# A graph network's first edge pass: three steps between the stages of the mixing, and products two tiles ahead of their sums

## The chip, the cores and the metric

One core of a Trainium2 chip runs the whole program. The metric is device time in microseconds for one execution. TensorE is called PE, VectorE DVE, ScalarE ACT, GpSimd POOL and SyncE SP, as in the profile.

## The reference, cut to what matters

Two layers over 3125 nodes with 256 features. Layer 0 is a max over edges, plus a linear attention ("mixing"), plus two chosen experts out of eight:

```python
xn = _layernorm(x)
# graph part: theta(x_dst - x_src) + phi(x_src), relu, segment_max over edges
e = relu((xn[dst] - xn[src]) @ theta_w.T + theta_b + xn[src] @ phi_w.T + phi_b)
gnn = segment_max(e, dst)
# mixing
q, k, v = split(xn @ W_qkv + b_qkv);  q2 = (q - mean(q))**2;  k2 = (k - mean(k))**2
k2 = l2norm_over_nodes(k2 / (sum(k2) + 1e-7));  q2 = l2norm(q2 / (sum(q2) + 1e-7))
mix = (v + q2 @ (k2.T @ v) / sqrt(N)) @ W_out + b_out
x = x + gnn + mix
x = x + layernorm(expert_mixture(layernorm(x)) + layernorm(x))
```

Layer 1 sums edges by relation, has another attention and another mixture of experts. The change does not touch it.

## The kernel before, in words

The nodes are 25 tiles of 128 rows, with the feature side transposed in `xT`. The program builds edge lists (to about 172 us), runs the first edge pass (172 to 1379 us), makes tables per relation, runs a second edge pass and ends with the experts of layer 1.

**The first edge pass** (`edge_pass`, line 1336, called at line 1956). For each tile POOL issues 22 to 45 indirect gathers (line 194), each of which brings one neighbour row for 128 nodes, in chunks of four that share one tile `gt` of a pool with six buffers. DVE takes the maximum of what came (line 1368), two rows at a time. The order of the instructions on DVE and POOL is the order in which the code issues them; PE and ACT are ordered by the scheduler.

**Background jobs.** All other work of layer 0 is cut into jobs with a cost each, in the deque `bg`. After each chunk of n gathers a credit grows by rate × n, the rate between 0.9 and 1.3 (what is left of costs over what is left of gathers), and jobs are taken while the credit is above zero. So the costs say only where, between which chunks, the instructions of a job stand. They are not times.

**The mixing.** `mix_tile` is a generator in three stages for each tile. Stage nought: PE projects q, k and v (lines 189, 1766, 1769) into PSUM tiles `mm` (four buffers), ACT copies v with the two means (`vs`, line 1774) and squares q and k with their sums in `ss` (lines 1775, 1776; `ss` is of the pool `small` with six buffers). Stage one: DVE inverts `ss` and scales k (lines 1778 to 1780), ACT squares for the norms (lines 1783 to 1786), PE accumulates `pkv` and `pnk` (lines 1788, 1792). Stage two: DVE scales q (lines 1794 to 1797), PE transposes it (line 1800), ACT copies it to `xt` (line 1801). The job `mix_step(i)` runs stage two of tile i-4, stage one of tile i-2 and stage nought of tile i. `nodes_in` jobs between them normalise the nodes (`xn`, line 172, pool `work` with two buffers) and transpose them (line 183, copied by ACT at 184). `mix_end` closes the mixing and makes `u_mix`.

**Products, sums, norms.** A group of one to three tiles (tiles 1, 2-3, 4-6, 7-9, 10-12, 13-15, 16-18, 19-21, 22-23, 24, then 0) has a `Fin0` object, whose jobs are added when the group's gathers are through. `products(j)` lets PE compute the node's own term into `po` (a tile `pt` of `ps_tr`, two buffers, shared with the transposes) and gnn and mixing terms into `pa` (`mm`). `sums(j)` lets DVE add them up (lines 1868 to 1871), with statistics. `norms` normalises the group (lines 1878 ff.), sums the means in `pmean` and transposes. Then come `hidden` (line 1526, gelu at 1530), `outputs_a` (lines 1552, 1555), `outputs_out` (copies by ACT, lines 1565, 1566) and `outputs_b` (DVE, lines 1574, 1575) of the two experts guessed from the first tiles. Routing (line 1453) and the checks on sorted edges (`redo`, line 1667) are jobs too. Tile 0 comes last and its products are at the end of the pass. "16-0" below is the chunk 0 of tile 16.

Of the kernel before, what the change touches and what calls it, by code (L numbers as in the profile page):

```python
# [11 lines left out]
F32 = mybir.dt.float32  # L12
# [8 lines left out]
P = 128  # L21
D = 256
NN = 3125
NT = 25
# [66 lines left out]
def rows(t):  # L91
    return LAST if t == NT - 1 else P
# [9 lines left out]
def gps_kernel(ctx: ExitStack, tc: tile.TileContext, a, out):  # L102
# [8 lines left out]
    ps_tr = ctx.enter_context(tc.tile_pool(name="ps_tr", bufs=2, space=PSUM))  # L111
    ps_acc = ctx.enter_context(tc.tile_pool(name="ps_acc", bufs=1, space=PSUM))
# [58 lines left out]
    def normalize(dst, src, mv, rs):  # L171
        V.tensor_scalar(dst, src, mv[:, 0:1], rs, op0=ALU.subtract, op1=ALU.mult)  # L172
# [7 lines left out]
    def to_xT(t, src):  # L180
        pt = ps_tr.tile([P, 2, P], F32, name="pt")
        for c in range(2):
            PE.transpose(pt[:, c, :], src[:, c * P : (c + 1) * P], ident)
        S.copy(xT[:, :, t * P : (t + 1) * P], pt)

    def tok_mm(ps, w, t, start=True, stop=True, lhs=None):
        lhs = xT if lhs is None else lhs
        for c in range(2):
            PE.matmul(  # L189
                ps, lhs[:, c, t * P : (t + 1) * P], w[:, c, :], start=start and c == 0, stop=stop and c == 1  # L190
            )
# [763 lines left out]
    with ExitStack() as prx:  # L955
# [204 lines left out]
        for j in range(LT // BLOCK):  # L1160
            pt = ps_tr.tile([P, 2, P], F32, name="pt")
# [157 lines left out]
    def fast():  # L1319
# [100 lines left out]
        pmean = [None]  # L1420
# [167 lines left out]
        with ExitStack() as l0x:  # L1588
# [128 lines left out]
            m0 = m0x.enter_context(tc.tile_pool(name="m0", bufs=2))  # L1717
# [42 lines left out]
            def mix_tile(t):  # L1760
                if t == 0:
                    pnk[0] = ps_acc.tile([P, D], F32, name="pnk", tag="acc1")
                r = rows(t)
                pq = ps_mm.tile([P, 512], F32, name="mm")
                tok_mm(pq, w_qkv[:, :, :512], t, stop=False)
                PE.matmul(pq, ones_row, b_qkv[:, :512], start=False, stop=True)
                pvv = ps_mm.tile([P, 512], F32, name="mm")
                tok_mm(pvv[:, : D + 2], w_qkv[:, :, 512:], t, stop=False)
                PE.matmul(pvv[:, : D + 2], ones_row, b_qkv[:, 512:], start=False, stop=True)
                ss = small.tile([P, 2], F32, name="ss")  # L1770
                q2 = m0.tile([P, D], F32, name="q2", bufs=5)
                k2 = m0.tile([P, D], F32, name="k2", bufs=4)
                vs = m0.tile([P, D + 2], F32, name="vs", bufs=4)
                S.copy(vs, pvv[:, : D + 2])
                S.activation(q2, pq[:, :D], AF.Square, bias=vs[:, D : D + 1], accum_out=ss[:, 0:1])
                S.activation(k2, pq[:, D:], AF.Square, bias=vs[:, D + 1 :], accum_out=ss[:, 1:2])
                yield
                V.tensor_scalar(ss, ss, 1e-7, None, op0=ALU.add)
                V.reciprocal(ss, ss)
                V.tensor_scalar(k2, k2, ss[:, 1:2], None, op0=ALU.mult)  # L1780
                sq = m0.tile([P, D], F32, name="sq")
                s4 = small.tile([P, 1], F32, name="s4")
                S.activation(sq, q2, AF.Square, scale=ss[:, 0:1], accum_out=s4)
                S.activation(s4, s4, AF.Sqrt)
                ksq = m0.tile([P, D], F32, name="ksq")
                S.activation(ksq, k2, AF.Square)
                for c in range(2):
                    PE.matmul(
                        pkv[:, c, :], vs[:r, c * P : (c + 1) * P], k2[:r, :],
                        start=(t == 0 and c == 0), stop=(t == NT - 1), skip_group_check=True,  # L1790
                    )
                PE.matmul(pnk[0], ones[:r, :], ksq[:r, :], start=(t == 0), stop=(t == NT - 1))
                yield
                V.tensor_scalar(s4, s4, 1e-12, None, op0=ALU.max)
                V.reciprocal(s4, s4)
                V.tensor_tensor(s4, s4, ss[:, 0:1], op=ALU.mult)
                V.tensor_scalar(q2, q2, s4, None, op0=ALU.mult)
                pt = ps_tr.tile([P, 2, P], F32, name="pt")
                for c in range(2):
                    PE.transpose(pt[:, c, :], q2[:, c * P : (c + 1) * P], ident)  # L1800
                S.copy(xt_q[:, t, :, :], pt)
# [41 lines left out]

            class Fin0:
                def __init__(self, tiles, accs):
                    self.tiles, self.accs, self.k = tiles, accs, len(tiles)
                    self.mv = small.tile([P, 4, 2], F32, name="mv1")
                    self.rs = small.tile([P, 4], F32, name="rs1")  # L1850
                    self.pa, self.po = {}, {}

                def products(self, j):
                    t = self.tiles[j]

                    po = self.po[j] = ps_tr.tile([P, D], F32, name="pt")
                    tok_mm(po, w_own, t)
                    pa = self.pa[j] = ps_mm.tile([P, 512], F32, name="mm")
                    tok_mm(pa, w_tm, t, stop=False)
                    for c in range(2):  # L1860
                        PE.matmul(
                            pa[:, D:], xt_q[:, t, c, :], u_mix[:, c, :], start=False, stop=False, skip_group_check=True
                        )
                    PE.matmul(pa, ones_row, b_tm, start=False, stop=True)
# [12 lines left out]
                def norms(self):  # L1877
                    V.reciprocal(self.rs[:, : self.k], self.rs[:, : self.k])
                    for j, t in enumerate(self.tiles):
                        if t in (1, SEEN + 1):  # L1880
                            pmean[0] = ps_acc.tile([P, 2], F32, name="pmean", tag=f"acc{1 + (t > 1)}")
                        normalize(xt_tok[:, t, :], x[:, t, :], self.mv[:, j, :], self.rs[:, j : j + 1])
                        V.tensor_tensor(x[:, t, :], x[:, t, :], bet, op=ALU.add)
                        r = rows(t)
                        for c in range(2):
                            PE.matmul(  # L1886
                                pmean[0][:, c : c + 1], xt_tok[:r, t, c * P : (c + 1) * P], ones[:r, 0:1],
                                start=(t in (1, SEEN + 1) and c == 0), stop=(t in (SEEN, 0)),
                                skip_group_check=True,
                            )  # L1890
                        to_xT(t, xt_tok[:, t, :])

                def jobs(self):
                    def step(i):
                        if i < self.k:
                            self.products(i)
                        if i > 0:
                            self.sums(i - 1)

                    out = [(5.0 if 0 < i < self.k else 2.5, lambda i=i: step(i)) for i in range(self.k + 1)]  # L1900
                    return out + [(2.0 * self.k, self.norms)]

            def staged(gen, costs):
# [3 lines left out]
            nodes = [staged(nodes_in(g), (1.0, 4.0) + 5 * (1.2,)) for g in range(5)]  # L1907
            bg.extend(nodes[0])
            mixing = [mix_tile(t) for t in range(NT)]

            def mix_step(i):
                for back in (4, 2, 0):
                    if 0 <= i - back < NT:
                        next(mixing[i - back], None)

            for i in range(NT + 4):
                bg.append((7.0 if i < NT else 3.0, lambda i=i: mix_step(i)))
                if i // 5 + 1 < 5:
                    a0, a1 = ((0, 1), (1, 2), (2, 3), (3, 5), (5, 7))[i % 5]
                    bg.extend(nodes[i // 5 + 1][a0:a1])  # L1920
# [262 lines left out]
        with ExitStack() as l1x:  # L2183
# [126 lines left out]
            class Group:  # L2310
# [174 lines left out]
                def step(self, i):  # L2485

                    self.take()
                    if i < NX:
                        self.hidden(i)
                    if 1 <= i <= NX:  # L2490
                        self.outputs(i - 1)
                    if i == NX + 1:
                        leaving.extend((tick[0] + 9, t) for t in self.tiles)
# [117 lines left out]
    with tc.If(unfit < 1):  # L2611
        fast()
# [78 lines left out]
```

## Time and profile before

| | us |
|---|---|
| median of three runs | 2949.89 |
| the runs | 2949.89, 2947.96, 2967.57 |
| the profiled execution | 2956.36 |
| its span, first to last instruction | 2954.5 |
| mean granted TensorE clock | 0.766 |

Busy time by stretch, in us, from the windows of the trace (POOL counts a gather's own time only):

| stretch, us | PE | DVE | ACT | POOL | granted clock |
|---|---|---|---|---|---|
| 172 to 490, mixing | 191.5 | 135.5 | 76.4 | 199.6 | 0.72 |
| 490 to 1379, rest of the first pass | 434.3 | 341.3 | 85.0 | 569.1 | 0.67 |
| 1379 to 1640 | 218.6 | 148.3 | 53.7 | 104.8 | 0.92 |
| 1640 to 2954 | 960.2 | 509.7 | 287.8 | 745.0 | 0.81 |

In a line of waits, "ss L1778 <- ACT k L1776: 76.2, 8, 21.3" says that the engine stood idle ahead of its instructions of line 1778, that the wait ended with ACT's instruction of line 1776, 76.2 us in 8 times, the longest 21.3. "remote" is a releaser that could not be told by line, "issue" time in which nothing shown was waited for. A line of the timeline has the start, the duration, engine, line, operation, tiles and in brackets the idle time ahead of it.

### The profile page before, as it was taken

The numbers are of one execution on the slowest core, as the hardware profiler recorded it, in microseconds if no ns is written. First come the engines' busy times: TensorE is split into PE (matmuls) and PEld (weight loads), VectorE is DVE, ScalarE is ACT, GpSimd is POOL, SyncE is SP. The second block draws the span as 40 slices with busy tenths as digits, with TensorE's granted clock in tenths as the row PEclk, the third lists the DMA queues.
The fourth block names the chain that finished last, engine by engine and source line by source line (L and its number), as shares of the span: only waits on it lengthen the run. The fifth ranks groups of instructions, "written<-read, shape, count | busy, mean of one in ns | idle before, by whom it ended". The sixth has DMA issues, their size and how long they took to land.

```text
span 2954.5 us, 21207 instructions
## 1 busy us (share of the span) xinstructions
PE 1868.2 (63%) x6161; PEld 1201.3 (41%) x6161; DVE 1227.5 (42%) x3400; ACT 556.2 (19%) x1308; POOL 1718.8 (58%) x1830
## 2 busy tenths in 40 slices
PE   4345666413574635374998267858886886766868
PEld 2223333202342313243443145645554565554657
DVE  7434434434433424334664243335343434343342
ACT  5212221001110101022221122122111122122233
POOL 5566666675667566653146645655666555665651
PEclk9667767655686657687998668878897887887979
DMA  6533333343334233332357432322332222232320
GB/s 180 135 91 86 94 85 104 94 108 101 90 87 107 74 90 85 92 78 58 148 211 237 135 97 75 91 80 84 89 92 85 84 82 79 82 89 73 86 72 18
DMA packets 125963, 290.10 MB, mean 98 GB/s; under 512 B 41386, under 2 KB 63982, under 8 KB 122632
## 3 DMA queue, kind: packets, MB, share of 16 engines
q0 software_dynamic: 83184, 230.02, 28.4%
q1 hardware_dynamic: 38122, 55.88, 5.6%
q10 hardware_dynamic: 4526, 2.71, 0.3%
q8 instruction: 52, 0.85, 0.1%
q14 instruction: 79, 0.65, 0.1%
HBM read 249.07 MB, written 39.41 MB: 98 GB/s over the span
## 4 chain that ended last, share of the span: by engine, by line
PE 25%; issue 9%; another core or an unknown queue 7%; DVE 5%; POOL 4%; ACT 2%; DMA 1%; ACTq 0%; DVEq 0%; SPq 0%; POOLq 0%
PE mm L2432 9%; PE py L2463 7%; PE mm L189 6%; POOL gt L194 4%; DVE gt L1375 1%; PE mm L2326 1%; DVE bnst L163 1%; PE pctx L2271 0%; PE mm L2324 0%; DVE x L2482 0%; PE py L2449 0%; PE pt L2402 0%; DMA gt<-htab_f,idx2g 0%; DVE acc L1377 0%
## 5 line engine op out<-in xcount | busy, mean ns | idle before, releaser
L194 POOL DMA_INDIRECT gt<-htab_f,idx2g x742 | 727.8, 981 | 497.2 <-DVE acc L1377 241.3
L194 POOL DMA_INDIRECT gt<-btab,idx x764 | 751.6, 984 | 389.5 <-issue 208.5
L2432 PE MATMUL mm<-xT,w 128*128 128x256 f32 (+4 forms) x1536 | 429.8, 434 | 107.4 <-issue 61.2
L2463 PE MATMUL py<-w,hT 128*128 128x256 f32 (+1 forms) x1600 | 407.8, 407 | 71.6 <-issue 45.5
L2432 PEld LDWEIGHTS mm<-xT,w 128*128 128x128 f32 x1536 | 294.5, 217 | 224.1 <-issue 121.9
L2463 PEld LDWEIGHTS py<-w,hT 128*128 128x128 f32 (+1 forms) x1600 | 319.8, 203 | 144.1 <-issue 78.9
L1368 DVE TENSOR_TENSOR run<-run,gt 128x512 f32<-128x512 f32 (+1 forms) x400 | 266.3, 666 | 169.6 <-DMA gt<-btab,idx 110.8
L2436 ACT ACTIVATE hT<-mm,b 128x256 f32<-128x256 f32 (+4 forms) x384 | 174.9, 476 | 584.9 <-remote 266.3
L2482 DVE SCALAR_TENSOR_TENSOR x<-py,wf,x 128x256 f32<-128x256 f32 x200 | 88.1, 477 | 440.0 <-remote 226.0
L1375 DVE TENSOR_TENSOR gt<-gt 128x512 f32<-128x512 f32 (+1 forms) x364 | 193.5, 531 | 14.2 <-DMA gt<-htab_f,idx2g 4.9
L1555 PE MATMUL mm<-w,hT 128*128 128x256 f32 x400 | 130.0, 471 | 106.2 <-issue 85.8
L189 PE MATMUL mm<-w_rel,xT 128*128 128x512 f32 x400 | 179.0, 605 | 7.1 <-issue 3.2
L1526 PE MATMUL mm<-xT,w 128*128 128x384 f32 (+2 forms) x320 | 113.8, 519 | 72.8 <-ACT y L1566 34.8
L1555 PEld LDWEIGHTS mm<-w,hT 128*128 128x128 f32 x400 | 90.6, 234 | 158.6 <-issue 123.9
L189 PEld LDWEIGHTS mm<-w_rel,xT 128*128 128x128 f32 x400 | 75.9, 193 | 102.2 <-issue 89.9
L1526 PEld LDWEIGHTS mm<-xT,w 128*128 128x128 f32 x320 | 69.4, 242 | 116.2 <-ACT y L1566 38.4
L1886 PE MATMUL pmean<-ones,xt 128*128 128x1 f32 (+1 forms) x100 | 21.3, 317 | 139.2 <-DVE xt L172 133.7
L189 PE MATMUL mm<-w_qkv,xT 128*128 128x512 f32 (+1 forms) x200 | 90.9, 579 | 25.7 <-issue 19.2
L194 POOL DMA_INDIRECT gt<-htab_f,soon x72 | 71.6, 995 | 44.7 <-issue 20.9
L189 PE MATMUL pt<-w_own,xT 128*128 128x256 f32 x100 | 42.0, 553 | 70.7 <-issue 37.0
L194 POOL DMA_INDIRECT run<-btab,idx x50 | 48.7, 973 | 64.2 <-DVE idx L1630 30.9
L1886 PEld LDWEIGHTS pmean<-ones,xt 128*128 128x128 f32 (+1 forms) x100 | 21.9, 300 | 148.3 <-DVE xt L172 140.9
(440 smaller groups left out, 2221.9 us busy)
## 6 DMA issues: line engine op xcount, KB each, us to landing
htab_f<-hs SPq DMA_DIRECT2D x25, 1024.0 KB
gt<-btab,idx POOLq DMA_INDIRECT x764
gt<-htab_f,idx2g POOLq DMA_INDIRECT x742
w<-in_f_W_dram SPq DMA_DIRECT2D x20, 512.0 KB
ntab<-x SPq DMA_DIRECT2D x5, 640.0 KB
btab<-bs SPq DMA_DIRECT2D x5, 640.0 KB
x<-in_x_dram SPq DMA_DIRECT2D x4, 640.0 KB
otab<-xn SPq DMA_DIRECT2D x16, 128.0 KB
```

The lines of the kernel that those rows point to most:

```text
L163: V.bn_stats(out=st, in_=src)
L189: PE.matmul(ps, lhs[:, c, t * P : (t + 1) * P], w[:, c, :], start=start and c == 0, stop=stop and c == 1)
L194: G.indirect_dma_start(out=dst, out_offset=None, in_=table, in_offset=bass.IndirectOffsetOnAxis(ap=idx, axis=0))
L1368: V.tensor_tensor(d, d, gt[:, k1 - b : k1 - a, :], op=op)
L1375: V.tensor_tensor(gt[:, :h, :], gt[:, :h, :], gt[:, m - h : m, :], op=op)
L1526: PE.matmul(ph[:, :n], w1[:, i, c, f * P : (f + 1) * P], xT[:, c, at0 : at0 + n], start=(c == 0), stop=(c == 1),)
L1555: PE.matmul(py[:, i * D : (i + 1) * D], hTs[i][:, f, j * P : (j + 1) * P], w2[:, i, f, :], start=False, stop=(f == FC - 1), skip_group_che ...
L1886: PE.matmul(pmean[0][:, c : c + 1], xt_tok[:r, t, c * P : (c + 1) * P], ones[:r, 0:1], start=(t in (1, SEEN + 1) and c == 0), stop=(t in ( ...
L2432: PE.matmul(ph[:, :n], w1s[e][:, c, f * P : (f + 1) * P], xT[:, c, at0 : at0 + n], start=(c == 0), stop=(c == 1),)
L2436: S.activation(hT[:, f, :n], ph[:, :n], AF.Gelu, bias=b1[:, e, f : f + 1])
L2463: PE.matmul(py[:r, j * D : (j + 1) * D], hT[:, f, at : at + r], w2s[e][:, f, :], start=(f == 0), stop=(f == FC - 1),)
L2482: V.scalar_tensor_tensor(d, y, wf[:r, t, e : e + 1], d, op0=ALU.mult, op1=ALU.add)
```

## The change

The stages of the mixing are three steps apart instead of two: `mix_step(i)` runs stage two of tile i-6, stage one of tile i-3, stage nought of tile i, and there are two steps more. `q2`, `k2` and `vs` get 8, 5 and 5 buffers. In `Fin0`, the first job issues the products of two tiles and each sum comes two products behind: a group of k tiles has k+1 jobs as before, now at 5.0 each (before: 2.5, then 5.0, the last 2.5). Every third `po` lies in the accumulators' pool with tag `acc2`, which is free after `mix_end`, and both `pmean` have the tag `acc1`.

```diff
-                q2 = m0.tile([P, D], F32, name="q2", bufs=5)
-                k2 = m0.tile([P, D], F32, name="k2", bufs=4)
-                vs = m0.tile([P, D + 2], F32, name="vs", bufs=4)
+                q2 = m0.tile([P, D], F32, name="q2", bufs=8)
+                k2 = m0.tile([P, D], F32, name="k2", bufs=5)
+                vs = m0.tile([P, D + 2], F32, name="vs", bufs=5)
...
+            pots = [0]
+
             class Fin0:
...
-                    po = self.po[j] = ps_tr.tile([P, D], F32, name="pt")
+                    pots[0] += 1
+                    if pots[0] % 3:
+                        po = self.po[j] = ps_tr.tile([P, D], F32, name="pt")
+                    else:
+                        po = self.po[j] = ps_acc.tile([P, D], F32, name="po", tag="acc2")
...
-                            pmean[0] = ps_acc.tile([P, 2], F32, name="pmean", tag=f"acc{1 + (t > 1)}")
+                            pmean[0] = ps_acc.tile([P, 2], F32, name="pmean", tag="acc1")
...
                     def step(i):
-                        if i < self.k:
-                            self.products(i)
-                        if i > 0:
-                            self.sums(i - 1)
-
-                    out = [(5.0 if 0 < i < self.k else 2.5, lambda i=i: step(i)) for i in range(self.k + 1)]
+                        for j in range(2) if i == 1 else (i,):
+                            if j < self.k:
+                                self.products(j)
+                        if i > 1:
+                            self.sums(i - 2)
+
+                    out = [(5.0, lambda i=i: step(i)) for i in range(1, self.k + 2)]
                     return out + [(2.0 * self.k, self.norms)]
...
-                for back in (4, 2, 0):
+                for back in (6, 3, 0):
...
-            for i in range(NT + 4):
+            for i in range(NT + 6):
```

## The prediction

> **What bounds the kernel now.** I read the page first, its busy shares and the costliest groups:
>
> ```profile
> PE 1868.2 (63%) x6161; PEld 1201.3 (41%) x6161; DVE 1227.5 (42%) x3400; ACT 556.2 (19%) x1308; POOL 1718.8 (58%) x1830
> L194 POOL DMA_INDIRECT gt<-btab,idx x764 | 751.6, 984 | 389.5 <-issue 208.5
> ```
>
> No engine is full over the whole span, so the stage decides. The change is in the first edge pass, 172 to 1379 us, whose work POOL issues: a gather every 0.98 + 0.30 = 1.25 to 1.28 us, some 66 of 80 possible in each 100 us. The gathers and node loads of the 1207 us make 1000; the other 208 are stalls. They end with VectorE (DVE), as POOL's waits from 170 to 1390 us say (total, times, longest):
>
> ```profile
> POOL gt L194 <- issue: 196.6, 644, 0.7
> POOL gt L194 <- DVE slots L1643: 81.3, 19, 11.4
> POOL run L194 <- DVE idx L1630: 25.5, 2, 21.0
> POOL run L194 <- DVE rs L1878: 19.3, 1, 19.3
> ```
>
> POOL may run six chunks of four gathers ahead, about 30 us; only when DVE is held longer does it stop. What holds DVE, same stretch:
>
> ```profile
> DVE ss L1778 <- ACT k L1776: 76.2, 8, 21.3
> DVE acc L1869 <- remote: 61.9, 5, 20.5
> DVE acc L1868 <- remote: 59.8, 4, 32.9
> DVE acc L1868 <- PE pt L189: 58.7, 4, 34.2
> DVE xt L1574 <- ACT y L1566: 50.1, 3, 20.6
> ```
>
> Line 1778 opens the second stage of the mixing; 1868 and 1869 are the sums that read the products. Both are what the change touches. I laid each POOL stall beside the DVE wait ahead of it in the timeline. Of the 208 us, 59.9 lie in the mixing (to 478 us), 83.3 behind waits of the sums, and 65 behind things the change leaves alone (routing, outputs_b, the redo flag). In the mixing, 39.7 follow a wait at 1778: 7.62 (at 238 us), 7.93 (284), 2.24, 6.42, 7.38, 7.03, 1.08; 8.13 (332) follows a wait for a normalised tile at line 172 and 12.03 (172) is the start.
>
> One such stall, in the timeline (start, duration, and in brackets the idle time before it):
>
> ```profile
> 288.49 0.38 ACT L1774 COPY vs<-mm 128x258 f32<-128x258 f32 x1 [17.04 <-remote]
> ...
> 290.09 0.17 DVE L1778 TENSOR_SCALAR ss<-ss 128x2 f32<-128x2 f32 x1 [21.32 <-ACT k L1776]
> ...
> 292.52 1.23 POOL L194 DMA_INDIRECT gt<-btab,idx  x1 [7.93 <-DVE idx L1630]
> ```
>
> ScalarE (ACT) waited for a product whose matmul was issued at 269.17: it was TensorE's finish that came 17 us late. Is TensorE short of work there, or slow? Its row for the mixing (PE, PEld, DVE, ACT, POOL busy, clock):
>
> ```profile
> 170.00:490.00 320.00, 191.49 (x532) 99.80 (x532) 135.60 (x466) 76.42 (x290) 200.94 (x204) 0.72 0.34 88
> ```
>
> Two of its waits from 175 to 490 us:
>
> ```profile
> PE pkv L1788 <- DVE k L1780: 14.1, 2, 13.7
> PE pnk L1792 <- ACT ksq L1786: 14.1, 2, 13.6
> ```
>
> It is 60% busy at a granted clock of 0.72, and in most of the rest it waits for operands that wait for its own late finishes. Only 14.1 + 14.1 = 28.2 us wait for the other half of the loop, which the change can bring forward.
>
> **The change, part by part.**
>
> *Mixing, three steps instead of two.* Nothing is added: 25 tiles, the same instructions. POOL's and SP's order does not change; only in the first pass do PE, ACT and DVE change order, so all later stages cost zero difference. Stage one of a tile comes three steps after its projections, stage two three after that. A step is paid 7.0 at a rate of 0.9 to 1.3 per gather, about two chunks or 8 x 1.25 = 10 us. So the wait at 1778 asks for a product that is 10 us older. Tile 9 of the timeline: DVE asked at 268.77; it would ask for tile 8, whose squares ended at 263.73, and go on. Every POOL stall behind 1778 is shorter than 10 us, so if TensorE catches up between its late spells, all 39.7 us go. If TensorE has no slack, the added step is spent once, 10 us. Between the ends I take 20: the row nearest is the 28.2 us that TensorE itself spends waiting for k and ksq, less part of it because both waits can be one spell seen by two lines. What is late next: line 172 has two buffers of xn, and a late transpose holds DVE there (29.6 us in 2 waits, 8.13 of it already in POOL). Queued behind that wait are DVE's max-additions and so POOL.
> A new wait comes with it: ss has six buffers and seven tiles are now live, so ACT's squares of tile i wait for DVE's stage two of tile i-6, in the same step. Behind them on ACT stand sq, ksq and the copies. TensorE's projection of tile i stands behind pkv of i-3, which needs that same DVE step, so this costs nothing while that order holds; if it fails, ACT loses one step's lead, at most the 10 us above. Larger buffers of q2, k2, vs cost no instruction. The two added steps carry 3.0 each, 6 credits or some 6 gathers, and lie beside gathers: zero, up to 7 us if mix_end comes late for the first sums.
>
> *Products two tiles ahead of sums.* Same matmuls. The first job now issues two tiles' products, each sum follows its own by a job more. The planner's jobs per chunk show products to sums one or two chunks (5 to 10 us) further apart for second and later tiles, none for the first tile of most groups: at starts of tiles 10, 16, 22 and 24 products and first sum share a chunk in both kernels. Against the waits (POOL stall behind each): 849 us, line 1869, 6.93, gain 5; 493 and 524 us, 7.04 and 7.49, gain 2.5 to 14, I take 8; 1204 to 1226, 10.20, gain 7; 1330, 11.38, gain 5. Sum 25, from 10 (the 7 and the 2.5 alone, about) to 45 (all of 7.0 + 7.5 + 6.9 + 10.2 + 11.4 = 43.0, and 2 at 1296).
> Against: a group of k tiles now costs 5(k+1) instead of 5k, so norms, hidden and outputs come one to three chunks later, 5 to 15 us. So outputs of tiles 10 to 12 (15-0 to 15-3 in tile and chunk) come nearer to the products of 16-0, which keep their place. That is the costliest stall today:
>
> ```profile
> 949.07 0.58 PE L1555 MATMUL mm<-w,hT 128*128 128x256 f32 x1 [1.80 <-issue]
> ...
> 951.87 0.58 PE L1555 MATMUL mm<-w,hT 128*128 128x256 f32 x1 [2.22 <-issue]
> ...
> 976.32 0.42 DVE L1868 TENSOR_TENSOR acc<-acc,pt 128x256 f32<-128x256 f32 x1 [34.17 <-PE pt L189]
> ```
>
> TensorE works off output matmuls at one per 2.80 us while the products stand behind them; POOL lost 20.96. Later outputs make this 0 to 15 longer; I take 8, since the group's own hidden matmuls also shift. At 24-0 (1274 us, 19.30 lost) I take 2 of 0 to 10. Net of this part: -25 + 10 = -15, from -45 to +15.
> The spare PSUM tile for every third po and one tag for both pmean: no instruction; with ps_tr shared with transposes it can only ease a wait, in the 1868 rows already counted; zero.
>
> *End of pass.* The last jobs stand at chunk 10 of tile 0 instead of 7; no gather is left behind them. DVE finished 1384.5 against POOL's last issue at 1377.95. From 0 to +10; I take +4, under one chunk.
>
> A rule weighed. Row: those matmuls run 0.58 us and are spaced 2.80 with work queued. The Trainium skill, "TensorE: Matmul & The Clock Gate", Part 1, says the clock halves after an idle window of about 3.4 us and comes back after as much busy time; by that, keeping TensorE fed would lift the 0.72 and all 39.7 of the mixing would go (total -51). But a halved clock makes at most two of one, not 2.80 of 0.58, and these spells come with a full queue, so a deeper queue need not cure them; my sum stays at 20.
>
> **Sum.** -20 - 15 + 4 = -31 on the profiled execution, 2956.4 (span 2954.5 and 1.9 around it): 2925. That execution lies 6.5 above the median 2949.9, inside the runs' 2948 to 2968; from the median the sum gives 2919. I say 2920.
>
> **Rivals.**
> 1. All lags absorbed. Mixing -40, sums -45, end 0: 2950 - 85 = 2865. For: every stall there is under 12 us, a step is 10. Against: 16-0 and 24-0 have no lag to gain.
> 2. TensorE is the limit, and the wait moves from 1778 to xn at 172 or to the next spell: -10, and the sums even out at 0: 2940 to 2950. For: 60% busy plus late finishes leave it little slack.
> 3. Slower: the outputs pushed toward a tile's first products. Place: 16-0 and 24-0. Price: 15 + 10 more stall, and 10 at the end, against 0 to 5 gained in the mixing: +30 to +35, 2980 to 2985; a third such place, a group that now meets outputs (stall like the 19.30), adds 20, 3005. It decides once DVE's waits at 1868 behind line 1555 pass some 100 us in the pass.
> 4. That the change does nothing: excluded in the order, but within the spread of 20 us between runs it is rival 2.
>
> **How the numbers follow.** Forecast (2900 to 2938) 0.42; rival 1 0.15; rival 2 0.20; rival 3 0.23. 1% (29.5 us) is about what can be told from no change: 2920 and 2979 bound it. Of the forecast 0.27 lies under 2920; with rival 1, faster 0.42. Of the forecast 0.15, and rival 2's 0.20, are same: 0.35. Rival 3: slower 0.23. The range of 8 in 10 leaves out the lower half of rival 1 and the upper half of rival 3: 2868 to 2985; the forecast's own is 2900 to 2938.
>
> **What would show it.** Right: the 1778 rows fall from 100 us to below 40; POOL's stalls to 478 us from 60 to about 40; PE's pkv<-k and ksq waits gone; DVE behind 1869 down from 76 (61.9 + 14.3). The last gather's issue, 1378 now, moves by the whole gain, and the stages after keep their length. Wrong: xn at 172 or 1868 behind line 1555 rising by as much as 1778 falls; the last gather at 1378 or later; or later stages moving although their order is the same.

## The result, and the profile after

The changed kernel is slower: median 3000.2 us of 12 runs against 2959.2 of 12 runs of the kernel before, ratio 1.0113 (95% interval 1.0083 to 1.0144). Measured a second time, beside other runs of the kernel before, it was 1.0101 (1.0069 to 1.0133). The ratios keep only the runs within 1.5% of the fastest run of their kernel, so they are not quotients of the medians (here 1.0139), and where one fast run of the kernel before (2907.3 us) made the rule drop most of its others, the ratio of medians is told beside it. The forecast of 2920 and its range (to 2985) were wrong; of the rivals, the third, with the side "slower", is the one that came.

The profiled execution took 3006.8 us, span 3004.9, 50.4 more than that of before. The page and POOL's waits, 170 to 1400 us (the pass ends 17 us later now):

```profile
PE 1894.5 (63%) x6161; PEld 1206.2 (40%) x6161; DVE 1227.5 (41%) x3400; ACT 556.9 (19%) x1308; POOL 1716.2 (57%) x1830
```

```profile
POOL gt L194 <- DVE slots L1643: 95.1, 15, 12.9
POOL run L194 <- DVE idx L1630: 79.6, 4, 31.6
```

The engines execute the same number of instructions (TensorE's busy time is 26 us longer, at a granted clock of 0.758 instead of 0.766); the waits of POOL for DVE are fewer (20 over 1.5 us, before 24) and longer, the longest 31.6 instead of 21.0. DVE's, in the same stretch (line 1874 is the old 1868, 1875 the old 1869):

```profile
DVE acc L1875 <- PE mm L1870: 95.7, 5, 45.3
DVE acc L1875 <- remote: 64.0, 4, 30.0
...
DVE xn L172 <- remote: 43.8, 2, 26.3
DVE acc L1874 <- remote: 39.1, 2, 20.3
DVE ss L1778 <- ACT k L1776: 37.3, 4, 21.4
DVE run L1380 <- ACT spill L1399: 33.8, 1, 33.8
DVE rs L1748 <- ACT rs L1746: 22.6, 2, 21.6
```

So the wait that the mixing part aimed at did fall, from 76.2 to 37.3. But line 172 rose from 29.6 to 43.8, and 22.6 at line 1748 is new (the standard deviation of the nodes, behind the same ACT queue). TensorE's row for the mixing hardly changed:

```profile
170.00:490.00 320.00, 183.51 (x540) 96.04 (x541) 136.97 (x473) 76.53 (x290) 197.67 (x201) 0.74 0.33 87
```

Where do the 50.4 us lie? From the start of the trace to the last gather of the pass 16.8: POOL's stalls up to 480 us are 61.4 instead of 57.2, from there to the last gather 152.8 instead of 143.6, and 2.3 came before the first gather. From the last gather to POOL's first in the second pass: 65.6 instead of 46.1, so 19.5. This stretch, from the last gather to POOL's first of the second pass, is called the end of the pass below. The remaining 14 lie in code whose order is the same in both: from POOL's first gather of the second pass to the last instruction it is 1522 us before and 1536 in the changed kernel. The profiles of the experiments below spread from 1509 to 1528 there (those of one chip that is faster left out), and the changed kernel's second profile has 1528. So these 14 are taken for spread; that they are is not shown.

The end of the pass, kernel before:

```profile
1424.03 0.94 POOL L194 DMA_INDIRECT xn<-htab_f,own_i  x1 [45.14 <-PE mm L189]
```

and changed:

```profile
1388.75 0.42 DVE L1380 TENSOR_TENSOR run<-run,spill 64x256 f32<-64x256 f32 x1 [33.81 <-ACT spill L1399]
...
1460.27 0.94 POOL L194 DMA_INDIRECT xn<-htab_f,own_i  x1 [64.62 <-PE mm L189]
```

DVE got free at 1388.75, six us before the last gather was issued. Only then could it add up what POOL had fetched, and on TensorE the outputs of tiles 22 and 23, then hidden, outputs and products of the last tiles were still to come. Before, DVE's last long wait ended at 1362.6, 15 us ahead of the last gather, with the outputs of 22 and 23 already done.

### The profile page after: what moved, and what is told of

Its sections match the earlier page's. It is cut to its first block, busy times and chain, and to the rows that moved or that the text cites. A ratio compares the mean times of both kernels' runs of the same rounds, so it can differ in the third digit from the quotient of the medians.

```text
span 3004.9 us, 21198 instructions
## 1 busy us (share of the span) xinstructions
PE 1894.5 (63%) x6161; PEld 1206.2 (40%) x6161; DVE 1227.5 (41%) x3400; ACT 556.9 (19%) x1308; POOL 1716.2 (57%) x1830
## 5 line engine op out<-in xcount | busy, mean ns | idle before, releaser
L2470 PE MATMUL py<-w,hT 128*128 128x256 f32 (+1 forms) x1600 | 415.6, 409 | 94.2 <-issue 72.9
L1526 PE MATMUL mm<-xT,w 128*128 128x384 f32 (+2 forms) x320 | 124.4, 549 | 102.2 <-issue 56.5
L194 POOL DMA_INDIRECT gt<-htab_f,soon x72 | 70.1, 973 | 46.7 <-issue 21.7
L184 ACT COPY xT<-pt 128x256 f32<-128x256 f32 x100 | 36.0, 375 | 267.3 <-remote 191.2
L1530 ACT ACTIVATE hT<-mm,b 128x384 f32<-128x384 f32 (+2 forms) x80 | 40.4, 518 | 234.8 <-remote 128.3
L1875 DVE TENSOR_TENSOR acc<-acc,mm 128x256 f32<-128x256 f32 x25 | 10.5, 421 | 173.2 <-PE mm L1870 107.8
```

The costliest lines, as they stand in the source:

```text
L194: G.indirect_dma_start(out=dst, out_offset=None, in_=table, in_offset=bass.IndirectOffsetOnAxis(ap=idx, axis=0))
L1526: PE.matmul(ph[:, :n], w1[:, i, c, f * P : (f + 1) * P], xT[:, c, at0 : at0 + n], start=(c == 0), stop=(c == 1),)
L1530: S.activation(hT[:, f, :n], ph[:, :n], AF.Gelu, bias=b1[:, i, f : f + 1])
L2470: PE.matmul(py[:r, j * D : (j + 1) * D], hT[:, f, at : at + r], w2s[e][:, f, :], start=(f == 0), stop=(f == FC - 1),)
```

## What the stalls are

Laying each long wait of DVE beside POOL's stalls showed what the prediction had missed. A late finish, in the changed kernel's timeline:

```profile
350.02 0.95 POOL L194 DMA_INDIRECT gt<-btab,idx  x1 [0.30 <-issue]
...
355.23 0.37 ACT L1774 COPY vs<-mm 128x258 f32<-128x258 f32 x1 [21.85 <-remote]
355.27 0.73 DVE L172 TENSOR_SCALAR xn<-x,mv,rs 128x256 f32<-128x256 f32 x2 [26.31 <-remote]
...
359.20 1.20 POOL L194 DMA_INDIRECT gt<-btab,idx  x1 [8.23 <-DVE kind L1651]
```

POOL's last gather ends at 350.97, when all its buffers are full. 4.3 us later, ACT's wait for TensorE ends. In the first pass of the kernel before, 15 of the 17 waits of DVE over 10 us ended while POOL stood, at the median 5.0 us after POOL had stopped (3.2 to 12.2); in the changed kernel 15 of 16, at the median 6.5 us after (3.6 to 27.9, the longest two at 16-0 and 24-0). This alone proves nothing, because a DVE that waits long enough stops POOL whatever it waits for. But it gives the theory tested below: TensorE's finishes are held while gathers are issued, and come when POOL stops (theory B). A held stretch then costs POOL the 5 us and DVE's catching up, some 8 us, however old the product is that DVE asks for.

Code that comes late does not end these waits: in the kernel before, a packet of the two queues that carry instructions landed in none of the 17 during the last 6 us, and in 15 of them not at all.

TensorE is not the only engine whose finishes are late, which the theory leaves out. From 229 to 243 us of the kernel before, DVE does the statistics of five tiles, and ahead of each line 164, whose input DVE's own line 163 has just made, it stands 1.6 to 3.0 us; the last of them ends 5.1 us after POOL's stop at 238.0:

```profile
234.70 0.18 DVE L164 BATCH_NORM_AGGREGATE mv<-bnst 128x2 f32<-128x6 f32 x1 [2.31 <-issue]
...
240.29 0.18 DVE L164 BATCH_NORM_AGGREGATE mv<-bnst 128x2 f32<-128x6 f32 x1 [3.01 <-issue]
```

In the run of the groups up to 16 to 18 on the faster chip (at the end of the experiments) the same instruction does not wait:

```profile
200.54 0.18 DVE L164 BATCH_NORM_AGGREGATE mv<-bnst 128x2 f32<-128x6 f32 x1
```

In the first pass of the kernel before, 44 waits of DVE over 0.5 us, 42.0 us in all, end with an instruction of DVE itself (in the profiles on the three other held chips 29 to 59). In the two runs on the faster chip and in the run without POOL's gathers there is none.

A second theory, A, says what the change loses by: credits. The products and sums of a group of k tiles cost 5(k+1) instead of 5k, so all later jobs stand later, behind more work of a held TensorE.

## The experiments

Ratios are to runs of the kernel before on the same chip, with the 95% interval. "Held" is a chip where finishes come late as above (the kernel before takes about 2960 us); four of the five chips of the experiments were held.

**The mixing part alone** (bufs 8, 5, 5; `(6, 3, 0)`; `NT + 6`).

> The mixing part alone (stages three steps apart, the larger buffers), products and sums as before. Theory A (the loss comes from the products part: expert matmuls later, so first products at tile starts wait longer): the time is that of before within 10 us. Theory B, of the stalls themselves (a late finish of TensorE ends only some 3 to 5 us after POOL has run out of buffers and stops issuing gathers, so each costs POOL 7 to 8 us whatever the lag): POOL's stalls up to 480 us stay at 55 to 65 us, and the waits move from line 1778 to line 172. Rival, the recorded prediction: a late finish has a length of its own, 20 us of stalls go, ratio 0.993.

Measured 1.0031 (0.9995 to 1.0067). POOL's stalls up to 480 us: 62.1. The waits at 1778 behind k fell to 33.6, those at 172 rose to 52.4, and 21.0 at line 1748 came up. The rival's ratio (0.993) lies below the interval and its 20 us of stalls did not go; both theories hold.

**The products part alone** (all the rest of the diff).

> The products part alone (two tiles ahead, 5.0 a job, the third po in the accumulators), the mixing as before. Theory A: all of the loss, ratio 1.008 to 1.014, with POOL stalls at the starts of tiles 16 and 24 longer by 5 to 15 us each and some 15 to 20 us more between the last gather and the first gather of the second pass. Rival: the loss is in the mixing, ratio 1.000.

Measured 1.0088 (1.0056 to 1.012), end of the pass 64.9 us, stalls at 16-0 and 24-0 of 25.8 and 32.5 (before 21.0 and 19.3). As theory A had it, though its profiled last gather was at 1378.6, no later than before.

**One line of it: the credits.**

```diff
-                    out = [(5.0 if 0 < i < self.k else 2.5, lambda i=i: step(i)) for i in range(self.k + 1)]
+                    out = [(5.0, lambda i=i: step(i)) for i in range(self.k + 1)]
```

> The kernel before with one edit: every job of products and sums costs 5.0, so a group costs 5(k+1) instead of 5k; products still one tile ahead. Theory A (the loss is that norms, hidden and outputs come later): the loss of the products part, ratio 1.006 to 1.012, with 15 to 20 us more between the last gather and the first of the second pass, where the output matmuls of tiles 22 and 23 now lie behind the last held stretch. Rival: the two-ahead order itself loses (the first sum waits for more products), ratio 1.000.

Measured 1.0104 (1.0077 to 1.0131), end of the pass 65.6 us, 16-0 at 30.7, and a third place of that size, 30.1 at 1249.68 us, where DVE waited for products at line 1869 (about there 10.2 before). Not one product was moved ahead, and the whole loss is there.

```profile
1467.28 0.94 POOL L194 DMA_INDIRECT xn<-htab_f,own_i  x1 [64.68 <-PE mm L189]
```

**Two tiles ahead, on the old budget.**

```diff
-                    out = [(5.0, lambda i=i: step(i)) for i in range(1, self.k + 2)]
+                    out = [(5.0 * self.k / (self.k + 1), lambda i=i: step(i)) for i in range(1, self.k + 2)]
```

> Products two tiles ahead with the third po in the accumulators, but each job at 5k/(k+1), so that a group costs 5k as before; mixing as before. Theory A: ratio 0.997 to 1.003, the end of the pass as before (46 us from the last gather to the first of the second pass). Rival (the order itself loses): ratio 1.006 to 1.012, with the waits at line 1875 of 45 us at the starts of tiles 16 and 24 still there.

Measured 1.0034 (1.0001 to 1.0067), end of the pass 46.7 us, but 24-0 stalled 43.4 us in the profile and 16-0 19.8. Between the two expectations: the order may lose a little, not the whole.

**The changed kernel with that same edit.**

> The changed kernel with one edit: each job of products and sums at 5k/(k+1), so a group costs 5k as before the change; mixing and two-ahead stay. Theory A (the later norms, hidden and outputs cost the time): most of the loss goes, ratio 1.002 to 1.007, what the mixing part alone (1.003) and two-ahead on the old budget (1.003) gave. Rival: the parts only lose together, ratio 1.009 to 1.014.

Median 2956.0 of 12 runs against 2955.8 of 23, 1.000; ratio 1.0062 (1.0022 to 1.0102); end of the pass 46.7 us. By the medians the loss is gone; by the ratio 0.6% are left of 1.0 to 1.1%, and its interval reaches the whole. The changed kernel with still fewer credits (4k, below) has a comparison without this doubt, and there the loss is gone.

**Products of a group's first tile issued 25 us earlier** (budget as before, one tile ahead):

```diff
+                g = next(g for g, ts in enumerate(GROUPS) if t in ts)
+                if i == 2 and t == GROUPS[g][-1] and 4 <= g < len(GROUPS) - 1:
+                    early[g] = Fin0(GROUPS[g], None)
+                    early[g].products(0, True)
```

> The kernel before with the products of each group's first tile (groups from tiles 10 to 12 on) issued in the third chunk of the group's last tile, some 25 us ahead of the first sum, in the PSUM tag that mix_end leaves free (both pmean then in acc1); costs as before. Theory A: the waits of line 1868 behind line 1555 at the starts of tiles 16 and 24 (34 and 22 us) shrink, POOL's stalls there from 21 and 19 to about 8 each (a held stretch still costs that much): 15 to 30 us faster, ratio 0.990 to 0.996. Rival: the wait only passes to the next thing that needs TensorE, ratio 0.998 to 1.003.

By medians 2957.6 against 2955.8, 1.001; ratio 1.0067 (1.0017 to 1.0118). 16-0 fell to 16.2, 24-0 rose to 39.5, and the end of the pass took 65.5 us although no cost was changed: DVE waited 20.5 us at line 1574 there. By both figures theory A's gain is not there, and by the medians the rival came: the wait passes on to the next thing that needs TensorE.

**The credits in the last three groups only** (19 to 21, 22 and 23, 24).

> The kernel before with the cost of 5.0 for all jobs of products and sums only in the groups 19 to 21, 22 and 23, and 24 (15 credits more in all). If the end of the pass carries most of the loss (the 19.5 us more between the last gather and the second pass): ratio 1.005 to 1.009. If the starts of tiles in the middle carry it: ratio 1.000 to 1.003.

By medians 2967.8 (6 runs) against 2955.8, 1.004; ratio 1.01 (1.0014 to 1.0187), too wide to decide. Measured again on another chip:

> The kernel before with 5.0 for all jobs of products and sums only in the groups 19 to 21, 22 and 23, and 24. Where before takes 2955 us: 1.003 to 1.009, with 60 us or more between the last gather of the first pass and the first of the second. Where nothing holds TensorE: 0.999 to 1.003, and 43 to 48 us there.

1.0024 (0.9989 to 1.006), with the long end both times (63.1 and 65.9 us):

```profile
1436.90 0.94 POOL L194 DMA_INDIRECT xn<-htab_f,own_i  x1 [64.91 <-PE mm L189]
```

**The credits in the groups up to 16 to 18 only.**

> The kernel before with 5.0 for all jobs of products and sums only in the groups up to 16 to 18. Where before takes 2955 us: if the loss adds up over the pass, ratio 1.004 to 1.008 with the end of the pass as before; if the end carries nearly all, 0.999 to 1.003. Where nothing holds TensorE: 0.999 to 1.001.

1.0067 (1.0038 to 1.0096), 16-0 at 30.7 and 24-0 at 34.7, and the short end:

```profile
1435.22 0.94 POOL L194 DMA_INDIRECT xn<-htab_f,own_i  x1 [45.51 <-PE mm L189]
```

Middle and end add up (0.0067 + 0.0024 = 0.0091) to about what the one line costs in all (0.0104), the middle with more of it. The end's 19 us are plain in each profile that has the late last groups, but in the total they are within what the interval allows to vanish; the run above with products issued earlier had the long end too and lost nothing by the medians.

**A cheaper budget, 4k, in the changed kernel** (`4.0 * self.k / (self.k + 1)`).

> The changed kernel with 4k credits for a group's products and sums. Where before takes 2955 us: theory A, no loss, 0.992 to 1.001; rival (5k was the best place), 1.003 to 1.008. Where nothing holds TensorE: 0.998 to 1.000.

1.0004 (0.9976 to 1.0033), end of the pass 44.2 us. Theory A's range holds and the rival is out: with the mixing and the products as changed, but fewer credits, the loss is gone. A gain does not show: earlier than before brings nothing.

**A higher rate of credits**, `(0.9, 1.7)`.

> The kernel before with the highest rate of credits at 1.7 instead of 1.3, so that jobs come earlier when there are many. Theory A turned round: jobs at the end of the pass come earlier, 5 to 15 us less between the last gather and the second pass or behind the last held stretch, ratio 0.995 to 0.999. Rival: jobs closer together put sums nearer to their products, waits at 1868 and 1869 grow, ratio above 1.003.

1.005 (1.0017 to 1.0084): the rival. mix_end came at 439 instead of 491 us, and the stalls up to 480 rose from 57.2 to 71.2; from there on they fell from 143.6 to 138.6, the end was 44.8 us. What is gained later is lost in the mixing.

**Four buffers of gathers instead of six.**

> The kernel before with four buffers of gathers in the first pass instead of six, so that POOL stops after 16 gathers ahead (about 20 us) instead of 24 (30 us). Theory B (TensorE's late finish is released by POOL's stop): the waits of DVE behind TensorE get shorter by about 10 us each (the longest at line 1778 from 21 to about 12), the release still comes 3 to 5 us after POOL stops, POOL's stall for each stays 7 to 8 us, and the time stays within 15 us of before. Rival C (a late finish has its own length, given from outside): DVE's waits stay at 15 to 30 us, each POOL stall grows by about 10 us, some 15 to 20 of them, 100 to 200 us slower.

1.0019 (0.9987 to 1.0051): 8 gathers or 10 us less of run-ahead cost POOL next to nothing (its stalls sum to 208 us in the profile, before 201), where rival C had 100 to 200 us more. Timeline:

```profile
350.15 0.38 ACT L1774 COPY vs<-mm 128x258 f32<-128x258 f32 x1 [18.26 <-remote]
...
351.75 0.17 DVE L1778 TENSOR_SCALAR ss<-ss 128x2 f32<-128x2 f32 x1 [25.09 <-ACT k L1776]
354.18 0.94 POOL L194 DMA_INDIRECT gt<-btab,idx  x1 [9.64 <-DVE has L1612]
```

POOL had stopped at 344.5; ACT's wait ended 5.6 us after, DVE's 7.2. Over the pass 13 of DVE's 15 waits over 10 us ended while POOL stood, at the median 4.8 us after it had stopped (before 5.0). So the release moved with POOL's stop, and rival C is out. One miss: the waits did not get 10 us shorter. The median of those over 10 us was 23.1 us (before 18.8), the longest 30.6 (before 34.2). Why they are not shorter is open. Eight buffers, the other side of this test, did not fit into the on-chip memory beside the other tiles, so more run-ahead was not measured.

**The same transfers without POOL.** On a held chip, SP issues plain transfers, so the maxima are over the wrong rows, and the program then went into a branch that no other run takes; its time (21549.5 us) says nothing, its first pass does.

```diff
-                        gather(dst, table, ids[:, U - 2 - k : U - 1 - k])
+                        if own is None:
+                            nc.sync.dma_start(dst, table[:P, :])
+                        else:
+                            gather(dst, table, ids[:, U - 2 - k : U - 1 - k])
```

> The kernel before, with the first pass's gathers replaced: SP issues a plain transfer of the first 128 rows of the table into the same place, 806 of the same size, and POOL issues none there. So the maxima are over the wrong rows; all other work stays. Theory B, narrow (it is POOL's issuing of gathers that holds TensorE's finishes): no wait of 10 us or more behind TensorE between 200 and the end of the pass. Rival D (the traffic or the load of the other engines holds it): waits of 10 to 30 us stay, some every 40 to 50 us.

The pass was over at 740 us instead of 1385. Its mixing (the stretch of the rows above), and DVE's longest waits up to its end:

```profile
170.00:490.00 320.00, 266.00 (x932) 158.70 (x930) 255.99 (x753) 91.02 (x298) 6.00 (x7) 0.90 0.62 185
```

```profile
DVE acc L1872 <- PE mm L1867: 37.3, 12, 19.3
DVE acc L1871 <- PE pt L189: 25.1, 4, 12.9
DVE ss L1781 <- ACT k L1779: 16.6, 8, 3.3
```

TensorE did 932 matmuls in the 320 us instead of 532, with the transfers at 185 GB/s instead of 88, and the longest wait at the mixing's line is 3.3. Two waits over 10 us are left (19.3 and 12.9), so "none" was too strong; the held stretches every 40 to 50 us are gone. Rival D is out: neither traffic nor a busy TensorE holds it. The run changes two things at once, the engine that issues and the kind of transfer (plain instead of indirect); which of them matters is not told apart.

**Two runs on a chip where nothing is held.** The groups up to 16 to 18, and the budget of 4k, were run on another chip as well:

> The kernel before with the cost of 5.0 for all jobs of products and sums only in the groups up to 16 to 18 (the complement of the run on the last three groups, by medians 1.004). If the loss adds up over the pass: ratio 1.004 to 1.008, and the end of the pass as before (46 us from the last gather to the first of the second pass). If the end carries nearly all: ratio 0.999 to 1.003.

> The changed kernel with each job of products and sums at 4k/(k+1): a group costs 4k, less than before the change (5k) and less than with it (5k+5), so norms, hidden and outputs come earlier; mixing and two-ahead stay. Theory A: no loss, ratio 0.992 to 1.001, end of the pass 46 us or less. Rival (5k was the best place already, sums now stand nearer to their products): ratio 1.003 to 1.008.

There the kernel before itself took 2455.3 us (median of 23 runs, 2450.5 to 2461.1). The ratios were 0.9996 (0.9987 to 1.0006) and 0.9989 (0.998 to 0.9999). In the first of them POOL, 170 to 1165 us, has no stall at all beyond its 0.3:

```profile
POOL gt L194 <- issue: 177.3, 582, 0.3
POOL gt L194 <- DVE run L1368: 23.1, 76, 0.3
```

and DVE waits for gathers, not for TensorE:

```profile
DVE run L1368 <- DMA gt<-btab,idx: 427.0, 257, 3.5
DVE ss L1778 <- ACT k L1776: 62.1, 6, 18.7
```

Its wait of 62.1 at line 1778 is nearly that of before (76.2), and costs POOL nothing: each of the six, the longest 18.7, ended before POOL's buffers were full, where in the trace of before four of the five waits of 12 to 21 us at this line ended only after POOL had stopped. The same credits in the middle groups that lose 0.67% on a held chip lose nothing here. The changed kernel as it is was sent for both cases,

> The changed kernel again. Where the kernel before takes about 2955 us: ratio 1.008 to 1.014 as first measured. Where nothing holds TensorE (before about 2455 us): theory A with B says that the loss is made of held stretches and work queued behind them, so ratio 0.998 to 1.002; a rival, that the later jobs at the end cost time by themselves, 1.003 to 1.008 (8 to 20 us).

and met a held chip (the 1.0101 told above). What the change does where nothing is held was not measured; with 4k credits it gains 0.1%.

## Why the prediction was wrong, step by step

- What bounds the kernel: right for what it read. POOL's stalls behind DVE, and DVE's waits behind TensorE, are where the pass loses its time.
- "if TensorE catches up between its late spells, all 39.7 us go ... the added step is spent once ... Between the ends I take 20": the failed step on the side of the gain. It took a late finish for a thing with its own length, which an older product could outlast, and sized the gain by TensorE's 28.2 us of waits for k and ksq. Those rows did fall, to 3.4:

```profile
PE pnk L1792 <- ACT ksq L1786: 2.1, 1, 2.1
PE pkv L1788 <- DVE k L1780: 1.3, 1, 1.3
```

  The rows of line 1778 fell as well, from 102.4 us to 37.3, so two signs that were to show the forecast right came without the gain. The mixing part alone gained nothing (1.0031, stalls 62.1 instead of 57.2). The finish comes when POOL stops, so DVE must be held somewhere until then: at 172 and 1748 once it is not at 1778. Rival 2 had that wait at 172, but even its 10 us of gain were not there. The 39.7 was too high besides: DVE's last waits ahead of the stalls of 7.62 and 2.24 are not at line 1778 but at lines 164 (the lines at 234.70 and 240.29 above) and 1368.
- The ss buffers: no wait for them is seen in the changed kernel's mixing; zero was right.
- "Sum 25" of gains at the sums: not there. Two tiles ahead on the old budget measured 1.0034, and with the mixing 1.000 by medians (ratio 1.0062).
- "Later outputs make this 0 to 15 longer; I take 8" at 16-0, "2 of 0 to 10" at 24-0: right in kind; 24-0 too small. POOL lost 27.0 and 31.6 there instead of 21.0 and 19.3, so 6.0 and 12.3; in the profile of the credits alone 30.7 and 28.2. These are single profiles: 24-0 lost 44.4 us in that of the changed kernel on the old budget, which is no slower by the medians. So that these two stalls carry the loss is likely, not shown.

```profile
993.89 0.42 DVE L1875 TENSOR_TENSOR acc<-acc,mm 128x256 f32<-128x256 f32 x1 [45.34 <-PE mm L1870]
```

  It is the wait shown before at 976.32 with 34.17; it now ends at the second half of the products.
- "I take +4" at the end of the pass, from 0 to 10: 19.5. This is the failed step on the side of the price: the term was sized by chunks of DVE; what stood there was a held stretch with a group's hidden and outputs still behind it. Together the terms had -45 of gains and +14 of price; in the profile the stalls of the mixing grew by 4.3, those behind 480 us other than the two above fell by 9.1, and the price was 37.8.
- The rule of the clock gate: the Trainium skill ("TensorE: Matmul & The Clock Gate", Part 1) would have the clock halved after idle windows. The granted clock of the mixing is 0.72 held and 0.77 where nothing is held, and the spacing of matmuls at line 1555 over 2 us occurs 29 times in the first pass of before and never in those two runs. A clock 7% higher does not make 0.58 us out of 2.80, so it was right not to build on the rule. The same page's caveat that trace events of this clock can be unreliable is not tested by a run here.
- Rival 3 named the places, the mechanism and, at 2980 to 2985 (3005 with a third place), nearly the size (2994 and 3000 measured). Its +30 to +35 us is what the ratio 1.0113 makes of 2959 (33). It had 0.23 because the credits were costed as 5 to 15 us of shift each, and not as what they decide: how much work of TensorE stands behind a held stretch.

## What to carry to other kernels

Before a deeper pipeline is credited with a wait, look at what ends the wait: here 15 of 17 ended some 5 us after POOL had stopped, and the end moved with POOL's stop; a wait with such an end passes to the next instruction that needs the late engine. A job's cost in a hand-made planner is a change of order for everything after it; here one constant lost the 1%, and the two features beside it moved the time by 0.3% each (0.7% at most by the intervals). Sum a change on an execution, then ask whether another chip has the stalls at all.

## What the runs showed of the hardware

- On four of five chips finishes of TensorE, and by up to 3.0 us those of DVE for itself, come late while POOL issues indirect gathers back to back; DVE's long waits end at the median 5.0 us after POOL stops. Transfers of the same size from SP did not do it where the gathers did (first pass over at 740 us), and on the fifth chip POOL's gathers do not do it either: 2455 us instead of 2957 for the same kernel. What makes the difference between the chips, and how POOL's gathers reach the other engines, stays open; no run here tells.
- On a held chip the shorter run-ahead is nearly free: 16 gathers instead of 24 changed the time by 0.2% (interval -0.1 to +0.5%).
